# A four-layer graph network on one core: a reordered first chunk, a fixed TensorE order in the third layer, and preparations in steps

## The chip, the core and the metric

The kernel runs on one core of a Trainium2 chip. The metric is device time in microseconds, from launch to end of the core's work; lower is better. The time before is a median of three executions. A core has five engines that run their own instruction streams and meet at semaphores: TensorE (PE in the profile, with its weight loads as PEld), VectorE (DVE), ScalarE (ACT), GpSimd (POOL) and SyncE (SP, which here only starts transfers).

## The reference

Four graph layers in a row on x (4096 nodes, 256 features) with an adjacency matrix adj (4096 x 4096, 0 or 1). Each is followed by a residual sum and a layer norm. Numbered from 0 as in the code:

```python
# layer 0: four heads of 64, additive attention
Wh = (h @ W).reshape(n, heads, d)
e = leaky_relu(s_i[:, None, :] + s_j[None, :, :], 0.2)   # s_i, s_j: Wh with the halves of a
alpha = softmax(where(adj == 0, -inf, e), axis=1)
out = elu(einsum('ijh,jhd->ihd', alpha, Wh))
# layer 1: four heads of scaled dot products, mask from edge.T, then attn @ v
scores = q @ k.T / sqrt(64) + (edge.T - 1) * 10000
# layer 2: as layer 0 with one head, slope 0.01
h = x @ W; e = e_src[:, None] + e_dst[None, :]
out = elu(softmax(where(adj > 0, leaky(e), -1e12), axis=1) @ h)
# layer 3: cosine attention
Qn = cos_normalize(x @ Wq.T); Kn = cos_normalize(x @ Wk.T)
att = softmax(where(adj > 0, Kn @ Qn.T, -9e15), axis=1)
out = 0.5 * (att @ x) + 0.5 * x
# every layer
x = layernorm(x + out)
```

The "third layer" of the change is layer 2.

## The kernel before

All is float32. The 4096 nodes are 32 tiles of 128 (NT) and 8 blocks of 512 (NB, each of QB = 4 tiles). x stays in SBUF as X for the whole kernel and is overwritten layer by layer. A layer first prepares each block (transpose, project, derive the factors), and then goes through units (b, j): for the 512 columns of block b and the neighbours of tile j, it makes attention weights `prob`, masked by adj (loaded on SP two or four tiles at a time), and multiplies them into the block's sums, which lie in PSUM over all 32 j (64 half tiles in layer 1). So a layer is a loop over 256 (512) units, and the preparations are woven into its first block.

**Additive layers (0 and 2).** exp(leaky(s_i + s_j)) is split into factors of i and j: `additive_values` multiplies a transposed block `xT` with the weights (L177), takes three exponentials on ScalarE (L181 to L183: `src`, `dst` and a column of V), and on VectorE writes the projected values, scaled by that column, to V (L184). `src` of a block is laid out as a row over all partitions. A unit is then a Relu on ScalarE of that row with `dst` as the scale (L261, L430), one VectorE instruction that adds 1 and multiplies with the mask (L264, L432), and the matmuls of `sums` (L274, L438).

**transposed_block** turns the four tiles of a block with TensorE into two PSUM banks (L118), which one copy each brings to SBUF (L120). `turn(b)` calls it.

**Layer 0's start** (in `additive_heads`). TensorE's order is the order in the code (`tc.manual_schedule`); the other engines' orders are made by the framework's planner from the same program order, its costs and what is ready. PSUM has two banks `g` from `bank()`, and two accumulators of three banks: `over` and `side`. `warm(2)` issues two products that nothing reads (L339). The row of `a` is spread over partitions in `side` (L342), and `attach` (VectorE, L108 and L110) extends the weights by it. Then come turn(0), warm(2) again, prepare(0) with tiles 0 to 2 in `side` and tile 3 in a bank, and the four rows of block 0 as transposes of broadcast columns (`first_rows`, L234) into a bank and the three banks of `over`. Unit 0's Relu reads the rows from PSUM, and `keep_rows` copies them to SBUF (L239, two on ScalarE, two on VectorE). turn(1) goes into two banks of `side`. The loop makes weights for unit i and sums for unit i - 2 (LAG = 2). After i = 0 stand turn(2) and prepare(1); after i = 3, 7, ... the next turn and preparation. The first sums need an accumulator, which takes the place of `over`. turn(b) also starts the load of x's block b + 2.

**Layer 1** ends with row sums collected in `den`: GpSimd adds even units' weights (L623), its DMA queue accumulates odd ones (L629), and `join_sums` (L646) adds the three parts. The last block's end is `tail`, which layer 2 calls with its own PSUM banks: joins on GpSimd, row sums by TensorE (L658) and copies of them (L661), transposes back (L666 for row sums, L673 for values), reciprocals, residual and layer norm.

**Layer 2** (`additive_one`). Four banks `g` and four accumulators acc0 to acc3; even blocks use the accumulators for their sums, odd blocks four `g`. Blocks 0 and 1 are prepared ahead of the loop; their rows are made by transposes (L420) and a copy (L421), those of later blocks by a trip through DRAM on GpSimd's queue (L415, L416). After weights j = 2, 6, ... of block 0 follow the turn and the preparation of the next block. Sums stand one unit behind weights. Layer 1's tail comes after the sums of unit 2. No engine has a fixed order here: the planner sets TensorE's too. `take_all` divides a finished block's sums, `outputs` finishes it in the next block.

**Layer 3** (`cosine_attention`) needs, for each block, normalised rows turned into T: `Cosine.prepare` turns the block, multiplies each tile with both weight matrices (L795, two tiles to a PSUM bank), takes squares with a running sum on ScalarE (L799), copies rows (L801), computes the inverse root, scales on VectorE (L806), transposes (L810) and copies to T (L811). Six of the eight are done during layer 2's last block, after j = 2, 6, ..., 22, in the banks acc0 to acc3 (`even_bank` gives them in turn), two during layer 3's first block. Its units are L834 (scores), L837 and L838 (exponential, mask) and L845 (sums).

Of the kernel before, what the change touches and what calls it, by code (L numbers as in the profile page):

```python
# [14 lines left out]
OP = mybir.AluOpType  # L15
# [13 lines left out]
def kernel(  # L29
# [140 lines left out]
    def additive_values(xT, b, groups, w_sb, V, src, dst, H, slope):  # L170

        g = 1.0 - slope
        heads = "p k (h d) -> p k h d"
        for k, n, pw in groups:
# [8 lines left out]
            nc.scalar.activation(V[:, t, D:], d, AF.Exp, scale=slope)  # L183
            nc.vector.tensor_tensor(V[:, t, :D].rearrange(heads, h=H), pw[:, :, :D].rearrange(heads, h=H),  # L184
# [12 lines left out]
    def additive_heads(a, H, slope, early, narrow, ahead):  # L197
# [7 lines left out]
        with ExitStack() as lay:  # L205
# [110 lines left out]
            def turn(b, bank=bank):  # L316
                if b + 2 < NB:
                    load_x(b + 2)
                busy = (nc.scalar.copy if b == 0 else nc.vector.tensor_copy,
                        nc.vector.tensor_copy if b == 1 else nc.scalar.copy)  # L320
                xTs[b] = transposed_block(sb, bank, b, busy)

            def prepare(b):
                groups = [(0, HC + 1, side), (HC + 1, 1, bank().rearrange("p (n f) -> p n f", n=1))]
                additive_values(xTs[b], b, groups, w_sb, V, src, dst, H, slope)
# [4 lines left out]
            with tc.manual_schedule(engines={mybir.EngineType.PE}):  # L330
# [14 lines left out]
                warm(2)  # L345
                prepare(0)
                banks = [bank()] + [over[:, h, :] for h in range(H - 1)]
                first_rows(banks)
                free = iter([side[:, 0, :], side[:, 1, :]])
                turn(1, lambda: next(free))  # L350
                for i in range(len(units) + LAG):
                    if i < len(units):
                        b, j = units[i]
                        weights(b, j, None if i else banks)
                        if (b, j) == (1, 4 * QB):
                            early()
                        if i % 8 == 4:
                            narrow(prob[b, j][:, 0, :1])
# [6 lines left out]
                    if i == 0 or i % QB == 3 and 3 + i // QB <= NB:  # L365
                        b = 1 if i == 0 else 2 + i // QB
# [15 lines left out]
    def additive_one(w_sb, slope, tail, op, follow):  # L382
# [3 lines left out]
        with ExitStack() as lay:  # L386
# [21 lines left out]
            def prepare(b, xT):  # L408
                groups = [(k, 1, bank().rearrange("p (n f) -> p n f", n=1)) for k in range(QB)]
                additive_values(xT, b, groups, w_sb, V, src, dst, 1, slope)  # L410
                part = row[:, b * QW:(b + 1) * QW]
# [47 lines left out]
            for b, xT in enumerate([turn(0), turn(1)]):  # L459
                prepare(b, xT)  # L460
            even = itertools.count()
            units = [(b, j) for b in range(NB) for j in range(NT)]
            for i in range(len(units) + 1):
                if i < len(units):
                    b, j = units[i]
                    weights(b, j)
                    if b == 0 and j % QB == 2 and j // QB + 2 < NB:
                        prepare(j // QB + 2, turn(j // QB + 2))
                if i:
                    b, j = units[i - 1]  # L470
                    sums(b, j)
                    if (b, j) == (0, 2):
                        tail(bank)
                        follow.start()
                    if b and j % 4 == 0 and j // 4 < QB:
                        outputs(b - 1, j // 4)
                    if b == NB - 1 and j in (6, 10, 14):
                        follow.load_mask(0, (j - 6) // 4, prob[b, j][:, :1])

                    if b == NB - 1 and j % 4 == 2 and j // 4 < NB - 2:  # L480
                        follow.prepare(even_bank, j // 4)
                    if j == NT - 1:
                        take_all(b)
# [7 lines left out]
    def multi_head_attention(w_sb, b_sb, tail, rows_of_den, narrow_edges):  # L491
# [12 lines left out]
        with ExitStack() as lay:  # L504
# [126 lines left out]
            def sums(b, j):  # L631
# [7 lines left out]
                if j == NH - 1:  # L639

                    kept[b] = [fin1.tile([P, QW], FP, name=f"kept{c}") for c in range(KC + 1)]
# [6 lines left out]
            def row_sums(bank, b):  # L648


                pds = [bank() for _ in range(KC)]
# [93 lines left out]
        def tail(bank):  # L745
            b = NB - 1
            join_sums(b, 1, nc.gpsimd)
            join_sums(b, 2, nc.gpsimd)
            row_sums(bank, b)
            reciprocals(turned_row_sums(bank, b), b)  # L750
            for k in (0, 2):
                half(turned_half(bank, b, k), b, k)
            mv = fin.tile([P, QB, 2], FP, name="mv")
            for k in range(QB):
                one_row(mv, k, X[:, b * QB + k, :D])
            layernorm_block(b, mv)
# [3 lines left out]
    class Cosine:  # L760
# [3 lines left out]
        def __init__(self, stack):  # L764
            self.stack = stack

# [17 lines left out]
        def prepare(self, bank, b):  # L784

            in_, w_sb, T = self.pool, self.w_sb, self.T
            xT = transposed_block(in_, bank, b)
            norm = in_.tile([P, QB, 2], FP, name="norm")
            rows = in_.tile([P, QB, 2, P], FP, name="rows")
            for k in range(QB):  # L790
                t = k % 2
                if t == 0:
                    pr = bank().rearrange("p (t n f) -> p t n f", t=2, f=P)
                for c in range(KC):
                    nc.tensor.matmul(pr[:, t, :, :], xT[:, c, k * P:(k + 1) * P], w_sb[:, c, :],  # L795
                                     start=(c == 0), stop=(c == KC - 1))
                for n in range(2):
                    sq = in_.tile([P, P], FP, name="sq")
# [171 lines left out]
```

## Time and profile before

| | us |
|---|---|
| median of three executions (2927.59 to 2929.03) | 2928.59 |
| the profiled execution | 2932.88 |
| its span, first to last instruction | 2931.0 |

| window, us | what runs | PE busy | DVE | ACT | POOL |
|---|---|---|---|---|---|
| 0 to 20 | layer 0's start | 16.88 | 6.84 | 8.02 | 0.70 |
| 20 to 40 | its first sums | 18.85 | 19.81 | 20.00 | 1.05 |
| 200 to 400 | layer 0's loop | 200.00 | 191.69 | 193.58 | 17.81 |
| 900 to 920 | layer 1's loop | 20.00 | 14.11 | 12.54 | 19.02 |
| 1724.5 to 1743.9 | layer 2's start | 17.48 | 11.67 | 10.20 | 5.51 |
| 2160 to 2237.8 | layer 2's last block, six preparations | 77.47 | 43.91 | 42.37 | 3.54 |
| 2246.8 to 2300 | layer 3's first units, two preparations | 52.78 | 27.80 | 20.83 | 2.96 |
| 2800 to 2931 | the end | 122.96 | 44.05 | 28.62 | 5.92 |

A row of a timeline gives the start, the length, engine, line, operation and the number of like instructions merged into it; in brackets is the idle time before it and what ended that. A float32 matmul appears as two instructions, a transpose as one. An instruction's end is modelled for TensorE and reaches past the start of the next by some 0.2 us, so lengths of neighbouring rows overlap; the distance from one row's start to the next is the time that it held the engine. Busy time therefore also holds short waits between instructions.

### The profile page before, as it was taken

The page shows a single profiled execution, that of the slowest core. Times are in us where ns is not written, and L with a number is a line of the kernel's source. Part 1 is how long each engine was busy: PE and PEld are TensorE (multiplying, and loading weights), DVE is VectorE, ACT ScalarE, POOL GpSimd, SP SyncE. Part 2 cuts the span into 40 slices and gives each one's busy share as a digit, 9 for nine tenths or more (in the row PEclk, how much of TensorE's full clock was granted, in tenths as well). Part 3 has the DMA queues.
Part 4 walks back from the last instruction along what each step waited for, and adds up shares of the span by engine and source line. Part 5 has one row for each costly group of instructions (what it writes and reads, how often), then busy time and mean ns, then how long its engine had stood idle before and what let it go on. Part 6 is the DMA issues. An engine that isn't in the chain of part 4 may idle for free.

```text
span 2931.0 us, 50407 instructions
## 1 busy us (share of the span) xinstructions
PE 2909.7 (99%) x20269; PEld 1560.3 (53%) x20269; DVE 1958.3 (67%) x2545; ACT 1668.9 (57%) x2613; POOL 926.6 (32%) x647
## 2 busy tenths in 40 slices
PE   9999999999999999999999999999999999999998
PEld 4333333333643333333333358888887777777776
DVE  8899999997677777877877865555555333333333
ACT  7899999997356666666666654444444222222222
POOL 0010010100078888888889850000000000000000
PEclk9999999999999999999999999999999999999999
DMA  7566666664068888889889876444442333333331
GB/s 203 102 138 139 136 141 141 137 131 84 1 147 191 183 185 190 182 185 195 176 187 188 180 161 137 151 152 151 154 132 52 51 58 58 58 58 58 58 58 29
DMA packets 207148, 374.94 MB, mean 128 GB/s; under 512 B 15057, under 2 KB 90817, under 8 KB 206018
## 3 DMA queue, kind: packets, MB, share of 16 engines
q0 software_dynamic: 102304, 177.77, 38.3%
q1 hardware_dynamic: 104336, 193.69, 20.1%
q8 instruction: 159, 2.61, 0.4%
q14 instruction: 75, 0.61, 0.1%
q10 hardware_dynamic: 274, 0.26, 0.0%
HBM read 317.07 MB, written 21.04 MB: 115 GB/s over the span
## 4 chain that ended last, share of the span: by engine, by line
PE 96%; DVE 2%; ACT 0%; DMA 0%; SPq 0%; issue 0%; DVEq 0%; ACTq 0%
PE acc L274 23%; PE acc L845 15%; PE p L604 14%; PE acc L637 14%; PE g L438 8%; PE acc L438 8%; PE p L834 4%; PE g L834 3%; PE g L532 2%; PE g L177 1%; PE pv L546 1%; PE acc L795 1%; PE g L118 1%; DVE prob L616 1%; DVE s L139 1%; PE acc L177 1%
## 5 line engine op out<-in xcount | busy, mean ns | idle before, releaser
L616 DVE TENSOR_TENSOR prob<-p,mask 128x1024 f32<-128x1024 f32 x512 | 622.8, 1222 | 197.4 <-ACT p L606 193.6
L606 ACT ACTIVATE p<-p,shift 128x1024 f32<-128x1024 f32 x512 | 556.3, 1088 | 331.8 <-PE p L604 331.0
L274 PE MATMUL acc<-prob,V 128*32 128x512 f32 x6144 | 664.0, 592 | 1.1 <-DVE prob L264 1.1
L623 POOL TENSOR_TENSOR den<-den,prob 128x1024 f32<-128x1024 f32 x248 | 618.5, 2494 | 72.1 <-DVE prob L616 62.7
L261 ACT ACTIVATE prob<-row,dst 128x512 f32<-128x512 f32 x1020 | 633.1, 712 | 0.1
L264 DVE SCALAR_TENSOR_TENSOR prob<-prob,mask 128x2048 f32<-128x2048 f32 x256 | 582.4, 2286 | 24.2 <-ACT prob L261 20.6
L604 PE MATMUL p<-qT,kT 64*64 64x512 f32 x4096 | 532.7, 591 | 5.5 <-DVE prob L616 5.5
L637 PE MATMUL acc<-prob,V 64*64 64x512 f32 x4096 | 531.4, 589 | 0.0
L845 PE MATMUL acc<-X,prob 128*128 128x257 f32 x2048 | 486.0, 380 | 0.0
L845 PEld LDWEIGHTS acc<-X,prob 128*128 128x128 f32 x2048 | 388.4, 190 | 162.2 <-issue 113.5
L838 DVE TENSOR_TENSOR prob<-prob,mask 128x512 f32<-128x512 f32 x256 | 176.3, 691 | 419.5 <-ACT prob L837 418.4
L274 PEld LDWEIGHTS acc<-prob,V 128*32 128x32 f32 x6144 | 197.3, 110 | 453.0 <-issue 433.5
L91 POOL COPY tick<-prob 128x1 f32<-128x1 f32 x35 | 39.7, 1133 | 1019.9 <-DVE prob L264 646.0
L430 ACT ACTIVATE e<-row,dst 128x512 f32<-128x512 f32 x256 | 184.3, 721 | 241.2 <-DVE prob L432 208.4
L637 PEld LDWEIGHTS acc<-prob,V 64*64 64x64 f32 x4096 | 155.8, 133 | 285.4 <-issue 278.2
L604 PEld LDWEIGHTS p<-qT,kT 64*64 64x64 f32 x4096 | 153.6, 133 | 284.4 <-issue 255.8
L432 DVE SCALAR_TENSOR_TENSOR prob<-e,mask 128x512 f32<-128x512 f32 x256 | 178.3, 696 | 174.7 <-PE acc L438 92.9
L782 POOL DMA_DIRECT2D mask<-in_adjT x64 | 47.4, 741 | 639.5 <-DVE prob L838 509.7
L629 POOL DMA_DIRECT2D den<-prob x240 | 225.2, 938 | 28.5 <-DVE prob L616 21.9
L837 ACT ACTIVATE prob<-p 128x512 f32<-128x512 f32 x144 | 85.8, 596 | 256.7 <-PE p L834 242.7
L438 PE MATMUL g<-V,prob 128*128 128x257 f32 x1024 | 226.6, 380 | 0.0
L438 PE MATMUL acc<-V,prob 128*128 128x257 f32 x1024 | 225.3, 380 | 0.0
(154 smaller groups left out, 1973.7 us busy)
## 6 DMA issues: line engine op xcount, KB each, us to landing
mask<-in_adjT SPq DMA_DIRECT2D x256, 512.0 KB
den<-prob POOLq DMA_DIRECT2D x240, 512.0 KB, 5.3
mask<-edges SPq DMA_DIRECT2D x256, 128.0 KB
mask<-in_adjT POOLq DMA_DIRECT2D x64, 512.0 KB, 5.7
edges<-in_adj POOLq DMA_DIRECT2D x32, 512.0 KB, 9.9
den<-prob SPq DMA_DIRECT2D x16, 512.0 KB
row<-far SPq DMA_DIRECT2D x7, 1024.0 KB
X<-in_x SPq DMA_DIRECT2D x7, 512.0 KB
```

Source lines behind the costliest of these rows:

```text
L261: nc.scalar.activation(z[:, h, :], r, AF.Relu, bias=-1.0, scale=dst[:, j, h:h + 1])
L264: nc.vector.scalar_tensor_tensor(z, z, 1.0, mask[m][:, j % MJ, :].unsqueeze(1).to_broadcast([P, H, QW]), OP.add, OP.mult)
L274: nc.tensor.matmul(acc[b][h * G:(h + 1) * G, n, :], part, prob[b, j][:, h, :], start=(j == 0), stop=(j == NT - 1))
L438: nc.tensor.matmul(acc[b][k][:, :D + 1], prob[b, j][:, k * P:(k + 1) * P], V[:, j, :], start=(j == 0), stop=(j == NT - 1))
L604: nc.tensor.matmul(p[c * d:(c + 1) * d, r, :], kT[half, c, j * d:(j + 1) * d], qT[half, c, cols], start=True, stop=True)
L606: nc.scalar.activation(p, p, AF.Exp, bias=shift)
L616: nc.vector.tensor_tensor(z, p, mask[m][:, j % MJ, :].unsqueeze(1).to_broadcast([P, KC, QW]), OP.mult)
L623: nc.gpsimd.tensor_tensor(to, to, flat, OP.add)
L629: nc.gpsimd.dma_start(to, flat, accum_op=OP.add)
L637: nc.tensor.matmul(acc[b][c][r * d:(r + 1) * d, :], V[half, j, r * d:(r + 1) * d], prob[b, j][half, r, :], start=(j == 0), stop=(j == NH - 1))
L834: nc.tensor.matmul(p, T[:, 0, j * P:(j + 1) * P], T[:, 1, cols], start=True, stop=True)
L845: nc.tensor.matmul(acc[b][k], prob[b, j][:, k * P:(k + 1) * P], X[:, j, :], start=(j == 0), stop=(j == NT - 1))
```

## The change

Three parts. In layer 0, turn(1) moves ahead of prepare(0) and into `over`, the second warm(2) is dropped, prepare(0)'s last tile goes to the third bank of `over`, the first rows take two banks `g` and two of `over`, turn(2) moves from behind unit 0 to behind unit 2's step, and the scaling of chunk 1's values is taken out of its preparation and put behind the weights of unit 1. In layer 2, TensorE's order becomes the program's, each turn moves two units ahead of its projection, the rows are filled in places of their own, and layer 1's tail is split into three calls after the sums of units 0, 3 and 5. Layer 3's preparation is split into three steps (turn; project and normalise; turn back), two and three units apart, and in the second step both tiles of a bank are multiplied before their squares.

```diff
-    def additive_values(xT, b, groups, w_sb, V, src, dst, H, slope):
+    def additive_values(xT, b, groups, w_sb, V, src, dst, H, slope, scaled=True):
...
+        if scaled:
+            scale_values(b, groups, V, H)
+
+    def scale_values(b, groups, V, H):
+        heads = "p k (h d) -> p k h d"
+        for k, n, pw in groups:
+            t = slice(b * QB + k, b * QB + k + n)
             nc.vector.tensor_tensor(V[:, t, :D].rearrange(heads, h=H), pw[:, :, :D].rearrange(heads, h=H),
                                     V[:, t, D:].unsqueeze(3).to_broadcast([P, n, H, D // H]), OP.mult)
...
-                busy = (nc.scalar.copy if b == 0 else nc.vector.tensor_copy,
-                        nc.vector.tensor_copy if b == 1 else nc.scalar.copy)
+                busy = (nc.scalar.copy if b == 0 else nc.vector.tensor_copy, nc.scalar.copy)
...
-            def prepare(b):
-                groups = [(0, HC + 1, side), (HC + 1, 1, bank().rearrange("p (n f) -> p n f", n=1))]
-                additive_values(xTs[b], b, groups, w_sb, V, src, dst, H, slope)
+            def prepare(b, last=None, scaled=True):
+                groups = [(0, HC + 1, side), (HC + 1, 1, last or bank().rearrange("p (n f) -> p n f", n=1))]
+                additive_values(xTs[b], b, groups, w_sb, V, src, dst, H, slope, scaled)
+                return groups
...
                 turn(0)
-                warm(2)
-                prepare(0)
-                banks = [bank()] + [over[:, h, :] for h in range(H - 1)]
+
+                free = iter([over[:, 0, :], over[:, 1, :]])
+                turn(1, lambda: next(free))
+                prepare(0, over[:, HC:, :])
+                banks = [bank(), bank(), over[:, 0, :], over[:, 1, :]]
                 first_rows(banks)
-                free = iter([side[:, 0, :], side[:, 1, :]])
-                turn(1, lambda: next(free))
                 for i in range(len(units) + LAG):
                     if i < len(units):
                         b, j = units[i]
                         weights(b, j, None if i else banks)
+                        if i == 1:
+                            scale_values(1, second, V, H)
...
-                    if i == 0 or i % QB == 3 and 3 + i // QB <= NB:
-                        b = 1 if i == 0 else 2 + i // QB
+
+                    if i == 0:
+                        second = prepare(1, scaled=False)
+                    elif i == 2:
+                        turn(2)
+                    elif i % QB == 3 and 2 + i // QB < NB:
+                        b = 2 + i // QB
                         if b + 1 < NB:
                             turn(b + 1)
                         prepare(b)
...
-            def prepare(b, xT):
-                groups = [(k, 1, bank().rearrange("p (n f) -> p n f", n=1)) for k in range(QB)]
+            def project(b, xT, ks=range(QB)):
+                groups = [(k, 1, bank().rearrange("p (n f) -> p n f", n=1)) for k in ks]
                 additive_values(xT, b, groups, w_sb, V, src, dst, 1, slope)
+
+            def fill_row(b):
                 part = row[:, b * QW:(b + 1) * QW]
...
-            for b, xT in enumerate([turn(0), turn(1)]):
-                prepare(b, xT)
...
+            with tc.manual_schedule(engines={mybir.EngineType.PE}):
+                xTs = {0: turn(0), 1: turn(1)}
+                project(0, xTs[0])
+                project(1, xTs[1], [0, 1])
+                fill_row(0)
+                project(1, xTs[1], [2, 3])
+                for i in range(len(units) + 1):
+                    if i < len(units):
+                        b, j = units[i]
+                        weights(b, j)
+
+                        if b == 0 and j // QB + 2 < NB:
+                            n = j // QB + 2
+                            if j % QB == 0:
+                                xTs[n] = turn(n)
+                            elif j % QB == 2:
+                                project(n, xTs[n])
+                                fill_row(n)
+                    if i:
+                        b, j = units[i - 1]
+                        sums(b, j)
+                        if (b, j) == (0, 1):
+                            fill_row(1)
+                        if b == 0 and j in (0, 3, 5):
+                            tail(bank, (0, 3, 5).index(j))
+                            if j == 5:
+                                follow.start()
+                        if b and j % 4 == 0 and j // 4 < QB:
+                            outputs(b - 1, j // 4)
+                        if b == NB - 1:
+                            if j in (6, 10, 14):
+                                follow.load_mask(0, (j - 6) // 4, prob[b, j][:, :1])
+
+
+                            for step, first in enumerate((0, 2, 5)):
+                                if j >= first and (j - first) % 4 == 0 and (j - first) // 4 < NB - 2:
+                                    follow.prepare(even_bank, (j - first) // 4, step)
+                        if j == NT - 1:
+                            take_all(b)
...
-        def tail(bank):
+        def tail(bank, step):
+
             b = NB - 1
-            join_sums(b, 1, nc.gpsimd)
-            join_sums(b, 2, nc.gpsimd)
-            row_sums(bank, b)
-            reciprocals(turned_row_sums(bank, b), b)
-            for k in (0, 2):
-                half(turned_half(bank, b, k), b, k)
...
+            if step == 0:
+                join_sums(b, 1, nc.gpsimd)
+                join_sums(b, 2, nc.gpsimd)
+            elif step == 1:
+                row_sums(bank, b)
+            else:
+                pd = turned_row_sums(bank, b)
+                pos = {k: turned_half(bank, b, k) for k in (0, 2)}
+                reciprocals(pd, b)
+                for k, po in pos.items():
+                    half(po, b, k)
...
-        def prepare(self, bank, b):
+        def prepare(self, bank, b, step):
...
+            if step == 0:
+                self.xT[b] = transposed_block(in_, bank, b)
+            elif step == 1:
...
+                for k in range(0, QB, 2):
                     pr = bank().rearrange("p (t n f) -> p t n f", t=2, f=P)
...
+                    for t in range(2):
+                        for c in range(KC):
+                            nc.tensor.matmul(pr[:, t, :, :], xT[:, c, (k + t) * P:(k + t + 1) * P], w_sb[:, c, :],
+                                             start=(c == 0), stop=(c == KC - 1))
+                    for t in range(2):
+                        for n in range(2):
+                            sq = in_.tile([P, P], FP, name="sq")
+                            nc.scalar.activation(sq, pr[:, t, n, :], AF.Square, accum_out=norm[:, k + t, n:n + 1])
+                    nc.vector.tensor_copy(rows[:, k:k + 2], pr)
...
+            steps = {(0, j + n): (NB - 2 + b, step) for b, j in enumerate((1, 12)) for step, n in enumerate((0, 2, 5))}
...
-                        co.prepare(bank, NB - 2)
-                    elif (b, j) == (0, 12):
-                        co.prepare(bank, NB - 1)
+                    if (b, j) in steps:
+                        co.prepare(bank, *steps[b, j])
```

## The prediction

> **What bounds the kernel.** I read the busy times first, then what TensorE waited for, then TensorE's timeline at the three places of the change.
>
> ```profile
> PE 2909.7 (99%) x20269; PEld 1560.3 (53%) x20269; DVE 1958.3 (67%) x2545; ACT 1668.9 (57%) x2613; POOL 926.6 (32%) x647
> ...
> PE g L177 <- DVE xT L120: 1.9, 1, 1.9
> PE acc L177 <- issue: 1.2, 1, 1.2
> PE acc L274 <- DVE prob L264: 1.1, 1, 1.1
> ```
>
> TensorE is busy 2909.7 of 2931.0 us, and the chain of waits gives it 96%. The change takes no computing from it except four warming instructions, so all it can win is TensorE's waits: 21.3 us in all, of which some 8 lie after the last matmul (2800 to 2931 us has 122.96 busy) and 5.5 in layer 1 (L604), both untouched. But the timeline models a matmul's end, and merged rows hide short waits; start minus start of successive rows shows them. The first chunk:
>
> ```profile
> 8.85 4.67 PE L177 MATMUL acc<-w_sb,xT 128*128 128x264 f32 x12 [1.19 <-issue]
> 13.36 1.05 PE L177 MATMUL g<-w_sb,xT 128*128 128x264 f32 x4
> ...
> 16.15 1.04 PE L118 MATMUL acc<-ident,X 128*128 128x128 f32 x8
> ...
> 18.57 2.94 PE L177 MATMUL acc<-w_sb,xT 128*128 128x264 f32 x12 [0.51 <-DVE xT L120]
> ...
> 22.32 2.78 PE L274 MATMUL acc<-prob,V 128*32 128x512 f32 x24
> 26.25 2.78 PE L274 MATMUL acc<-prob,V 128*32 128x512 f32 x24 [1.15 <-DVE prob L264]
> ...
> 33.55 0.64 PE L274 MATMUL acc<-prob,V 128*32 128x512 f32 x4
> ```
>
> From the third sum (33.55) TensorE waits for nothing until 680 us, so what the chunk gains before 33.55 shifts all that follows.
>
> **First chunk.** From the end of the first rows (16.15) to 33.55 are 17.40 us. Work in it: three turns of 0.87 (16.15 to 17.02), two preparations of 16 instructions at 0.222 (13.36 to 14.25 is four), 3.55 each, two sums of 2.61 (96 instructions take 10.44): 14.93. So 2.47 are waits: xT's copies, the row copies, prob.
> - *turn(1) moved ahead of prepare(0).* TensorE has a hole from 7.66 to 8.85: L177 writes the bank that attach's second product (DVE, to 8.75) still reads. Its X block is the next transfer after X(0) and w0; 1.3 MB at the measured 280 to 340 GB/s puts it at about 7 us. Eight transposes at half speed (0.21 each, as at 5.26) then end near 9.1: prepare(0) starts 0.25 later, and 0.87 leaves the later stretch. Its two load issues on SP (0.5 each) go ahead of masks first needed near 19 us; cost nothing.
> - *The second warm(2) removed.* Its 1.06 us stood in that hole: nothing by itself.
> - *The clock.* Twelve L177 take 4.51 us here and 2.77 at 18.57: the slow start costs 1.74, and the profile's clock row, which shows full speed, misses it. A rule speaks against the change: the Trainium skill, "TensorE: Matmul & The Clock Gate", Part 4 "PE-mode transpose", says that transposes don't count as activity for the clock gate. By it, warming begins with the L177 as before: 0, and in the worst case, with the two products missed, slow until 16.15, which adds four L177 at 0.22 and 16 transposes at 0.107, +2.6. If transposes do warm, work without a hole from 7 us brings full speed up to 1.85 us earlier: -0.9. The row is nearer the rule (transposes and products from 4.2 to 7.7 had not raised it by 8.85): I take 0.
> - *turn(2) behind the first sum, scaling of chunk 1 behind the second weights.* Work after 16.4 is now 14.06, so without a wait the third sum starts at 30.46 (-3.1). Waits: the four Relu at 0.62 end at 17.8, prob(0,0) takes 2.28 to 20.1, a row copy 0.68 behind it frees the accumulator: first sum at 20.8 (TensorE is there at 19.95). turn(2)'s second bank is the one that the deferred scaling still reads (0.94 and 0.41 on DVE). If DVE scales in the gap before prob(0,1), that is done by 22.1, the turn follows the sum (23.4 to 24.3), prob(0,1) is ready at 24.4, and with 2.61 + 0.87 + 3.55 the third sum starts at 31.5. If prob(0,1) goes first (ScalarE readies it at 21.4: 17.8, two row copies of 0.6, four Relu), scaling ends at 25.0, TensorE stands behind turn(2), and it is 32.5 (-1.1). In before DVE put the scaling first (22.73, then prob at 23.92): I take **-2.0**.
>
> **Start of layer 2 (the diff's third layer).**
>
> ```profile
> 1737.22 1.03 PE L438 MATMUL acc<-V,prob 128*128 128x257 f32 x4
> 1740.11 3.91 PE L177 MATMUL g<-w_sb,xT 128*128 128x258 f32 x16 [1.85 <-DVE xT L120]
> ...
> 1736.55 2.81 DVE L432 SCALAR_TENSOR_TENSOR prob<-e,mask 128x512 f32<-128x512 f32 x1 [1.14 <-PE acc L438]
> 1739.28 0.68 DVE L120 COPY xT<-g 128x512 f32<-128x512 f32 x1
> ...
> 1736.46 2.34 POOL L646 TENSOR_TENSOR den<-den 128x1024 f32<-128x1024 f32 x1 [7.60 <-DMA den<-prob]
> ```
>
> The longest wait: xT(2)'s copy stood on DVE behind a prob of 2.81 us, elsewhere 0.69, held as long as POOL's join of layer 1's row sums ran. With turn(2) at unit 0 and its project at unit 2 the order is project(1) to 1733.75, transposes to 1734.6, copy by about 1735.5, ahead of the join, under sum 0 (1.74 us, to 1736.4). First row: fill_row(0) ends at 1732.0, then ACT copy 0.58, Relu 0.72, prob 0.69 and hand-overs: 1734.3, under project(1)'s last half (1.74) and the turn (0.87); without that cover it would be 2.3. The blocked prob is then prob(0,1) or later, wanted after project(2) at 1739.9. Saved: 1.85 with 0.26 of slow first matmuls, and 0.33 of split fill_row(1): **-2.4** (ends -2.6 and -1.6, if sum 0 waits 0.8).
> A second rule to weigh: the same skill, "SBUF — State Buffer", "Who interferes with whom", has a DVE operation with two SBUF inputs and a GpSimd one shut each other out entirely. The joins move from unit 2 to unit 0; by the rule alone they could now meet prob(0,0), +2.1. The POOL row decides: the second join idled 7.60 us for its DMA, so being asked earlier doesn't move it. I take 0.
> *Tail in steps.* Row sums (16 matmuls, 0.59) now stand behind sum 3, near 1746, in a queue with every later sum behind them; the join ends at 1738.8, so no wait. Transposes come two units (3.5 us) after the kept copies (0.37 each), which stalled TensorE 0.36: **-0.4**. follow.start's two SP loads move from unit 2 to 5; wanted 400 us later: 0. Turns of blocks 3 to 7 go two units ahead of their projections; these already run without a wait.
>
> **Layer 3's preparations.**
>
> ```profile
> 2162.05 3.23 PE L795 MATMUL acc<-w_sb,xT 128*128 128x256 f32 x12
> 2165.12 1.46 PE L438 MATMUL g<-V,prob 128*128 128x257 f32 x6
> 2166.58 1.13 PE L795 MATMUL acc<-w_sb,xT 128*128 128x256 f32 x4
> 2167.54 4.50 PE L438 MATMUL g<-V,prob 128*128 128x257 f32 x20
> ```
>
> At 0.217 an instruction, 12 L795 should take 2.60; to the next row are 3.07 (0.47 lost), then 1.46 for 1.30 (0.16), 0.96 for 0.87 (0.09), and to the transposes at 2172.09 4.55 for 4.34 (0.21); with 0.19 before it 1.12 us. The second preparation (2173.43 to 2185.99) loses 0.81 in the same way, the other four some 0.75 each: 4.9. Its cause: the second tile's matmuls write a bank whose first half the Squares read. Now both tiles are multiplied before the Squares, and each step stands 2 or 3 units (3.5 to 6.1 us) behind its input: copies need 0.7, the root and scaling 4.45 (2167.5 to 2171.95). Step 0 at unit 0 writes acc0 and acc1, free at 2154.74 and 2155.46, before 2156.7. A wait or bank change per step stays, 0.1 each as in L177's runs, 0.25 a preparation: 4.9 - 1.5 = 3.4, taken as **-3.2** (ends -4.3 and -1.6, half). The two preparations inside layer 3 lose 1.0 and 0.6 (2250.34 to 2263.98, 2282.57 to 2293.68): **-1.0**. TensorE's order is not fixed there.
>
> **Sum:** -2.0 - 2.4 - 0.4 - 3.2 - 1.0 = -9.0. The profiled execution takes 2932.88 us with a span of 2931.0; less 9.0 it is 2923.9. It stands 4.3 above the median 2928.59, from which I forecast **2919.6 us**.
>
> **Rivals.**
> - *Half of it stays.* If the first chunk stands behind turn(2) and the small losses belong to every change of operand: 1.1 + 2.0 + 1.6 = 4.7 saved, 2923.9. For it: L177 keeps 0.1 in runs that wait for nothing. Against: the 0.47 are too large for that.
> - *More than that.* Transposes warm (0.9), the chunk runs free (another 1.1), the six preparations give 4.3: 3.1 more, 2916.5. For it: the free sum is 30.46.
> - *Slower: the fixed order makes every unit of layer 2 wait.* Its 256 sums stand one unit behind their weights; a wait costs a first matmul 0.10 us even where it is short. All of them: 26.6 - 9.0, +17.6, 2946.2; it turns slower beyond 0.2% from 143 waiting units. Against: L432's idle of 174.7 us is mostly for L438, so prob is ready as early as three buffers allow.
>
> **How the numbers follow.** A measurement tells 0.2% (5.9 us, below 2922.7) from nothing. Forecast 0.64, half 0.16, more 0.12, slower 0.05, no visible effect 0.03. Faster: 0.64 + 0.12 + 0.04 of the half case = 0.80; same 0.15; slower 0.05. The range reaches from the larger case to the half one: 2916.3 to 2924.6.
>
> **What would show it.** The third L274 group starting near 31.5 instead of 33.55; no wait for xT at the first L177 behind a turn in layer 2; sixteen L795 in one row of about 3.6 us; L666 without its 0.2. Wrong if TensorE waits at turn(2) for the scaling, at layer 2's first sum, or at unit 0 of its last block.

## The result, and the profile after

| | before | after | ratio after/before (95%) |
|---|---|---|---|
| first group, 6 runs each: median (lowest to highest), us | 2928.45 (2927.59 to 2930.18) | 2920.95 (2918.87 to 2921.23) | 0.9973 (0.996 to 0.9986) |
| later, on another chip, 22 and 5 runs | 2930.39 (2928.39 to 2932.99) | 2919.40 (2918.30 to 2921.02) | 0.9963 (0.9951 to 0.9976) |
| the profiled execution, us | 2932.88, span 2931.0 | 2920.96, span 2918.0 | |

The forecast was 2919.6 us with a range of 2916.3 to 2924.6. The kernel is faster, by 7.5 us in the first group and 11.0 in the second, where the steps added up to 9.0. The total is right, but the parts are not: they missed in both directions, and the runs below say which. So the closeness of the total is partly luck.

First the page of the changed kernel, its row of busy times, then what TensorE waited for (engine, line and buffer; releaser; us in total, times, longest):

```profile
PE 2900.7 (99%) x20265; PEld 1564.3 (54%) x20265; DVE 1957.0 (67%) x2544; ACT 1668.5 (57%) x2614; POOL 928.3 (32%) x647
```
```profile
PE p L635 <- DVE prob L647: 5.6, 8, 0.8
...
PE acc L280 <- DVE row L245: 1.0, 1, 1.0
```

The span is 13.0 us shorter, but TensorE's idle time fell only from 21.3 to 17.3 (2918.0 - 2900.7). The other 9.0 us left the *busy* time, with four instructions fewer. Slow first matmuls, matmuls at a low clock and stalls inside a merged row all count as busy, so a list of waits would have shown less than a third of this gain. Of the waits shown before, xT's 1.9 us at the projection is gone; layer 1's eight waits (now L635) are what they were.

TensorE's timeline of the first chunk in the changed kernel (start, busy time, line, what is computed; the sums are now at L280, the projections at L176):

```profile
7.41 1.97 PE L118 MATMUL acc<-ident,X 128*128 128x128 f32 x8 [0.40 <-DMA X<-in_x]
9.17 4.84 PE L176 MATMUL acc<-w_sb,xT 128*128 128x264 f32 x16
...
20.52 2.78 PE L280 MATMUL acc<-prob,V 128*32 128x512 f32 x24 [1.01 <-DVE row L245]
23.24 1.10 PE L118 MATMUL g<-ident,X 128*128 128x128 f32 x8
24.26 2.78 PE L280 MATMUL acc<-prob,V 128*32 128x512 f32 x24
...
31.56 8.79 PE L280 MATMUL acc<-prob,V 128*32 128x512 f32 x80
```

The third sum starts at 31.56, against 33.55 before and 31.5 forecast. One wait is left, 1.01 us ahead of the first sum, for the last row copy.

The same view where layer 2 starts (sums L453), and in its last block (layer 3's preparations L836):

```profile
1732.70 1.90 PE L453 MATMUL acc<-V,prob 128*128 128x257 f32 x8
1734.44 3.66 PE L176 MATMUL g<-w_sb,xT 128*128 128x258 f32 x16
1737.93 1.90 PE L453 MATMUL acc<-V,prob 128*128 128x257 f32 x8
```
```profile
2167.36 3.62 PE L836 MATMUL acc<-w_sb,xT 128*128 128x256 f32 x16
2170.81 3.63 PE L453 MATMUL g<-V,prob 128*128 128x257 f32 x16
```

In both, the next row starts when the work of the one before is done: 16 L176 in 3.49 us, 16 L836 in 3.45. The sixteen L836 were rows of 12 and 4 with sums between; now they are one row and cost 0.216 us each, what they cost with nothing lost.

For every profile I took the length of each stage, from the start of TensorE's first instruction in it to the first of the next. "Full clock" is the time of the trace's clock record, from which an L177 (L176) takes 0.22 us instead of 0.44. In e_chunk and e_pairs layer 2 has the order of before; the experiments are described below.

| profile | full clock from | first weights start | third sum starts | layer 2 to its last block | last block | layer 3 |
|---|---|---|---|---|---|---|
| before | 12.43 | 8.85 | 33.55 | 430.40 | 91.98 | 684.15 |
| before again (e_before) | 9.10 | 7.67 | 31.31 | 430.15 | 91.99 | 684.04 |
| after | 11.42 | 9.17 | 31.56 | 426.54 | 86.71 | 682.14 |
| after again (e_after) | 8.77 | 8.82 | 30.09 | 426.54 | 86.71 | 682.14 |
| e_chunk | 10.39 | 9.12 | 31.02 | 428.30 | 91.99 | 684.09 |
| e_rest | 9.14 | 8.05 | 31.53 | 426.54 | 86.71 | 682.29 |
| e_rest_again | 12.76 | 9.03 | 33.81 | 426.54 | 86.71 | 682.14 |
| e_pairs | 9.55 | 7.95 | 31.68 | 428.29 | 90.35 | 683.35 |
| e_unpaired | 10.46 | 8.95 | 30.97 | 426.54 | 101.93 | 682.91 |
| e_late_turn | 11.35 | 9.22 | 31.55 | 428.25 | 86.71 | 682.14 |
| e_no_fixed | 13.89 | 9.68 | 33.03 | 426.54 | 86.71 | 682.14 |
| e_turn1_back | 9.01 | 7.86 | 31.21 | 426.54 | 86.71 | 682.14 |
| e_rows_scaled | 11.02 | 9.11 | 31.41 | 426.54 | 86.71 | 682.14 |

The stages behind the first chunk repeat to 0.15 us wherever the program and its waits are the same. From the third sum to layer 2 all profiles take 1690.96 to 1691.07 us, but for e_before (1691.55, with 0.6 more of waits in layer 1), so what the chunk gains is kept. The first chunk itself does not repeat.

### The profile page after: what moved, and what is told of

It reads as the page before. It is cut to its first block, busy times and chain, and to the rows that moved or that the text cites. A ratio compares the mean times of both kernels' runs of the same rounds, so it can differ in the third digit from the quotient of the medians.

```text
span 2918.0 us, 50372 instructions
## 1 busy us (share of the span) xinstructions
PE 2900.7 (99%) x20265; PEld 1564.3 (54%) x20265; DVE 1957.0 (67%) x2544; ACT 1668.5 (57%) x2614; POOL 928.3 (32%) x647
## 4 chain that ended last, share of the span: by engine, by line
PE 98%; DVE 2%; ACT 0%; DMA 0%; issue 0%; SPq 0%; DVEq 0%; ACTq 0%
PE acc L280 23%; PE acc L888 15%; PE p L635 15%; PE acc L668 14%; PE acc L453 8%; PE g L453 8%; PE p L877 4%; PE g L877 3%; PE g L563 2%; PE g L176 1%; PE pv L577 1%; PE acc L176 1%; PE g L118 1%; PE acc L836 1%; DVE prob L647 1%; DVE s L139 1%
## 5 line engine op out<-in xcount | busy, mean ns | idle before, releaser
L280 PE MATMUL acc<-prob,V 128*32 128x512 f32 x6144 | 664.0, 592 | 1.0 <-DVE row L245 1.0
L635 PE MATMUL p<-qT,kT 64*64 64x512 f32 x4096 | 532.8, 590 | 5.6 <-DVE prob L647 5.6
L280 PEld LDWEIGHTS acc<-prob,V 128*32 128x32 f32 x6144 | 197.3, 110 | 452.2 <-issue 434.1
L445 ACT ACTIVATE e<-row,dst 128x512 f32<-128x512 f32 x256 | 184.2, 721 | 232.8 <-DVE prob L447 206.6
L635 PEld LDWEIGHTS p<-qT,kT 64*64 64x64 f32 x4096 | 153.8, 133 | 284.4 <-issue 255.7
L453 PE MATMUL g<-V,prob 128*128 128x257 f32 x1024 | 225.6, 380 | 0.0
L453 PE MATMUL acc<-V,prob 128*128 128x257 f32 x1024 | 225.1, 380 | 0.0
```

The costliest lines, as they stand in the source:

```text
L280: nc.tensor.matmul(acc[b][h * G:(h + 1) * G, n, :], part, prob[b, j][:, h, :], start=(j == 0), stop=(j == NT - 1))
L453: nc.tensor.matmul(acc[b][k][:, :D + 1], prob[b, j][:, k * P:(k + 1) * P], V[:, j, :], start=(j == 0), stop=(j == NT - 1))
L635: nc.tensor.matmul(p[c * d:(c + 1) * d, r, :], kT[half, c, j * d:(j + 1) * d], qT[half, c, cols], start=True, stop=True)
```

## The experiments

**Before, once more.** The same kernel, to see which of its rows belong to the program and which to one execution.

> The kernel before once more, for a second profile of it. The first profiled execution was 4.4 us above the median, and stage by stage it is 13.0 us longer than the profile of after, where the medians differ by 7.5. If the losses belong to the program, this profile shows them again: a prob of some 2.8 us behind the join, 0.47 lost in the first twelve L795 of a preparation, 522 us from layer 2's first transpose to layer 3's first score, and a span near 2931. If the first profile caught a chance (the join meeting a prob), the blocked prob and its 1.85 us wait are gone, and the span is near 2926.5.

It took 2930.91 us, with a span of 2929.0, between the two that were expected. Rows of its first chunk on TensorE's timeline:

```profile
7.67 3.62 PE L177 MATMUL acc<-w_sb,xT 128*128 128x264 f32 x12 [0.15 <-issue]
...
24.02 2.78 PE L274 MATMUL acc<-prob,V 128*32 128x512 f32 x24 [1.15 <-DVE prob L264]
...
31.31 1.92 PE L274 MATMUL acc<-prob,V 128*32 128x512 f32 x16
```

The third sum is at 31.31 here, not 33.55, in the same program. The first weights started 1.18 us sooner, and twelve of them took 3.45 us instead of 4.51, since the clock rose at 9.10 instead of 12.43. So 33.55, from which the prediction counted, was a late start. The wait at layer 2's start, in contrast, came back. First VectorE, then GpSimd, then TensorE in this run:

```profile
1734.90 2.56 DVE L432 SCALAR_TENSOR_TENSOR prob<-e,mask 128x512 f32<-128x512 f32 x1 [1.14 <-PE acc L438]
1737.38 0.68 DVE L120 COPY xT<-g 128x512 f32<-128x512 f32 x1
```
```profile
1734.55 2.35 POOL L646 TENSOR_TENSOR den<-den 128x1024 f32<-128x1024 f32 x1 [7.27 <-DMA den<-prob]
```
```profile
1738.20 3.91 PE L177 MATMUL g<-w_sb,xT 128*128 128x258 f32 x16 [1.60 <-DVE xT L120]
```

The prob ends at 1737.46, 0.56 us after the join (1736.90); the copy starts behind it; TensorE waits 1.60.

**The first chunk alone.** Layers 2 and 3 are those of before; only the diff's part in additive_values and additive_heads is kept.

> Only the first chunk is changed. Forecast's step: third sum near 31.5 us instead of 33.55, -2.0 us, 2926.4. If TensorE stands behind turn(2): -1.1. If the shift is lost later in layer 0 or 1, the third sum is early and the time as before.

2929.15 us (2927.51 to 2933.10), ratio 0.9996 (0.9988 to 1.0004): 1.3 us by the means, 1.6 by the medians, not told from nothing. Its layer 2 start shows something else. VectorE, then GpSimd:

```profile
1734.13 0.69 DVE L445 SCALAR_TENSOR_TENSOR prob<-e,mask 128x512 f32<-128x512 f32 x1 [1.14 <-PE acc L451]
1734.74 0.68 DVE L120 COPY xT<-g 128x512 f32<-128x512 f32 x1
```
```profile
1734.72 2.35 POOL L659 TENSOR_TENSOR den<-den 128x1024 f32<-128x1024 f32 x1 [7.86 <-DMA den<-prob]
```

Here the join came 0.59 us *after* the prob started, which took its usual 0.69, and the projection waits for nothing. That is why this stage takes 428.30 and not 430.15, with layer 2 as in before: whether the 1.6 to 1.9 us are lost hangs on when one DMA lands. Of four profiles with this layer 2, two lost them (e_pairs, below, did not).

**Layers 2 and 3 alone.** The first chunk is that of before.

> Only layers 2 and 3 are changed. Forecast's steps: -2.4 - 0.4 - 3.2 - 1.0 = -7.0, 2921.4. If the stages of the two profiles are taken at their word: -11, 2917.4. From the measured 7.5 in all, less 2.0 for the chunk: -5.5, 2923.

2919.80 us (2918.89 to 2920.24), ratio 0.9962 (0.9949 to 0.9976). This is 11.0 below before, what the stages of the two profiles said, so nearly the whole gain lies here. VectorE at layer 2's start, then TensorE:

```profile
1732.89 0.68 DVE L120 COPY xT<-g 128x512 f32<-128x512 f32 x1
...
1735.01 2.51 DVE L434 SCALAR_TENSOR_TENSOR prob<-e,mask 128x512 f32<-128x512 f32 x1 [0.25 <-ACT e L432]
```
```profile
1732.62 1.90 PE L440 MATMUL acc<-V,prob 128*128 128x257 f32 x8
1734.36 3.66 PE L177 MATMUL g<-w_sb,xT 128*128 128x258 f32 x16
```

A prob is held here too (2.51 us), but the copy of xT went 2 us before it, and TensorE loses nothing. The collision is still there; what moved is the work that stood behind it.

**Pairing alone.** Before, with one edit in Cosine.prepare; no steps, no hand-written order:

```diff
-            for k in range(QB):
...
+            for k in range(0, QB, 2):
...
+                for t in range(2):
+                    for c in range(KC):
...
+                for t in range(2):
+                    for n in range(2):
+                        sq = in_.tile([P, P], FP, name="sq")
+                        nc.scalar.activation(sq, pr[:, t, n, :], AF.Square, accum_out=norm[:, k + t, n:n + 1])
```

> Before, with one edit: both tiles of a bank are multiplied ahead of their Squares; the preparation stays one call and TensorE's order the planner's. If the bank that the Squares read is the cause, the first eight L795 of a preparation run without loss, some 0.5 us for each of eight preparations: -3 to -4. If the losses come from the weaving of sums between them, or from every change of operand: 0 to -1.

2927.76 us (2926.32 to 2929.45), ratio 0.999 (0.9983 to 0.9996). The last block is shorter by 1.64 us (91.99 to 90.35), layer 3 by another 0.7: 2.3, where 3 to 4 were expected. TensorE's timeline of the last block:

```profile
2158.10 3.98 PE L794 MATMUL acc<-w_sb,xT 128*128 128x256 f32 x16
2161.91 6.23 PE L438 MATMUL g<-V,prob 128*128 128x257 f32 x28
...
2170.46 3.80 PE L794 MATMUL acc<-w_sb,xT 128*128 128x256 f32 x16
```

The sixteen are in one row, yet it takes 3.98 and 3.80 us, not 3.62, and this run's list of waits has four for the scaled rows at the transposes back:

```profile
PE acc L809 <- DVE rows L805: 0.9, 4, 0.2
```

The steps still stand too close to what they read. Of the 5.28 us that the whole change wins in this block, pairing by itself gives 1.64; the other 3.64 came only with the steps set apart as well.

**The whole change and e_rest again**, side by side on another chip.

> The whole change once more, beside its second part alone on the same chip. If the chunk's 2.0 us add to the rest: 2.0 below the second part alone. If they came from the first profile's late w0 (prepare(0) began at 8.85 there, at 7.67 to 8.05 in three later profiles of the same chunk, at 9.12 and 9.17 behind the moved turn(1)): within 1 us of it.

> Second part alone, on the same chip as the whole change. It was 11.0 below before in the last group; expected again 9 to 11 below before, and either 2 above the whole change (chunk adds) or within 1 us of it (chunk gives nothing).

2919.40 (2918.30 to 2921.02) and 2920.00 us (2919.17 to 2922.00), ratios 0.9963 (0.9951 to 0.9976) and 0.9964 (0.9951 to 0.9978): the first chunk's new order shows as 0.6 us between these two, which lies within their scatter. TensorE at the start of the whole change's second profile:

```profile
5.53 1.54 PE L118 MATMUL g<-ident,X 128*128 128x128 f32 x6 [0.63 <-DMA X<-in_x]
7.11 1.88 PE L118 MATMUL acc<-ident,X 128*128 128x128 f32 x8
8.82 3.73 PE L176 MATMUL acc<-w_sb,xT 128*128 128x264 f32 x16
12.38 1.19 PE L240 MATMUL g<-ident,src 128*128 128x128 f32 x8
```

The sixteen L176 take 3.56 us, full speed from the first; in the other profile of this program (9.17 to 13.85) they take 4.68.

**turn(1) back behind the first rows**, in the new chunk. It should start prepare(0) sooner and keep the rest.

```diff
-                free = iter([over[:, 0, :], over[:, 1, :]])
-                turn(1, lambda: next(free))
+                warm(2)
                 prepare(0, over[:, HC:, :])
...
+                free = iter([side[:, 0, :], side[:, 1, :]])
+                turn(1, lambda: next(free))
```

(The copies of xT for block 1 are both on VectorE again.)

> The whole change, but turn(1) goes back behind the first rows (into side, both copies on VectorE) with warm(2) in the hole again; turn(2) stays behind the first sum. If waiting for X's second block ahead of prepare(0) is what eats the chunk's gain, prepare(0) begins near 8.0 instead of 9.15 and the third sum near 30.5: 0.5 to 1 below the whole change. If turn(1)'s place in the hole is what gains: 0.9 above it.

2920.09 us (2919.42 to 2920.75), ratio 0.9965 (0.9952 to 0.9977): no better than e_after (2919.40). TensorE's timeline:

```profile
7.86 4.36 PE L176 MATMUL acc<-w_sb,xT 128*128 128x264 f32 x16 [0.26 <-issue]
...
16.42 2.94 PE L176 MATMUL acc<-w_sb,xT 128*128 128x264 f32 x12 [1.38 <-DVE xT L120]
...
31.21 5.36 PE L280 MATMUL acc<-prob,V 128*32 128x512 f32 x48
```

prepare(0) does start at 7.86, and the gain is spent at once: prepare(1) waits 1.38 us for xT, whose copies are back on VectorE's path. Either order has one wait of over 1 us, the other one ahead of the first sum.

**Squares directly behind each tile's matmuls**, with the steps and their distances as changed (the two loops over t are one again).

> The whole change, but in a preparation's second step each tile's Squares follow its matmuls again, so the bank's second tile waits for the first one's Squares, now with TensorE's order fixed. If that bank is the cause of the losses: twice some 0.6 to 0.7 us for each of six preparations, +7 to +8, and a little in layer 3. If the distance between the steps did it: within 1 us of the whole change.

2935.62 us (2934.55 to 2936.86), ratio 1.0016 (1.0009 to 1.0023): this one edit turns the gain into a loss. The waits, then TensorE's timeline of one preparation:

```profile
PE acc L836 <- ACT sq L840: 12.0, 12, 1.3
```
```profile
2168.74 1.03 PE L836 MATMUL acc<-w_sb,xT 128*128 128x256 f32 x4
2171.05 2.00 PE L836 MATMUL acc<-w_sb,xT 128*128 128x256 f32 x8 [1.28 <-ACT sq L840]
2173.82 1.13 PE L836 MATMUL acc<-w_sb,xT 128*128 128x256 f32 x4 [0.77 <-ACT sq L840]
```

The second tile's matmuls stand until ScalarE has squared the first's, twice in a preparation. From 2168.74 to the next row (2174.79) are 6.05 us where 3.45 are work: 2.6 lost, by six preparations 15.6, and the stage is 15.2 longer. I had expected half of that. The named waits (1.28 + 0.77) are 2.05 of the 2.6. Of the rest, 0.2 are the two first matmuls behind a wait (each holds TensorE for 0.32 us instead of 0.22), and some 0.33 are the ends of the matmuls ahead of the waits, which are modelled too late and so count as busy. In before, the order that the planner had found put sums between the tiles (the rows of 12, 6, 4, 20), and the whole loss was 0.88 a preparation. That it is the fixed order that takes this cover away is likely but not shown: no run has this edit with the order left to the planner.

**The order not fixed in layer 2.** The program text stays in its new order; the planner orders TensorE's work again.

```diff
-            with tc.manual_schedule(engines={mybir.EngineType.PE}):
+            with nullcontext():
```

> The whole change, but in layer 2 TensorE's order is left to the planner again; turns, rows, tail and preparation steps stay where the change puts them. If fixing the order matters for itself: the losses of layer 2's last block come back in part, 2 to 4 us above the whole change. If the placing of the steps in the program did it: within 1 us of it.

2920.41 us (2919.04 to 2922.05), ratio 0.9965 (0.9952 to 0.9979), and the same 426.54, 86.71 and 682.14 us. With the steps in these places, fixing TensorE's order earns nothing more; the places in the program do it.

**turn(2) right ahead of project(2)** instead of two units before:

```diff
-                            if j % QB == 0:
+                            if j % QB == 0 and n > 2:
                                 xTs[n] = turn(n)
                             elif j % QB == 2:
+                                if n == 2:
+                                    xTs[n] = turn(n)
                                 project(n, xTs[n])
```

> The whole change, but turn(2) of layer 2 stands right ahead of project(2) again, with TensorE's order fixed. Forecast's step: the distance between turn and projection is the gain. TensorE then waits for xT(2)'s copies, at least 0.8 us, and up to 2.9 where the copy stands behind a prob that the join holds: 1 to 3 above the whole change. If the distance is worth nothing: no wait for xT in layer 2 and the same time.

2921.67 us (2920.15 to 2922.73), ratio 0.997 (0.9959 to 0.9982); the stage is 1.71 longer. TensorE at layer 2's start:

```profile
1732.35 2.00 PE L453 MATMUL acc<-V,prob 128*128 128x257 f32 x8 [0.41 <-DVE prob L447]
1734.18 1.04 PE L118 MATMUL g<-ident,X 128*128 128x128 f32 x8
1735.89 3.85 PE L176 MATMUL g<-w_sb,xT 128*128 128x258 f32 x16 [0.67 <-ACT e L445]
```

Without the transposes ahead of it the first sum waits 0.41 us for prob. The projection waits 0.67 us while the copies of its xT stand behind other work: VectorE's behind a prob (copy to 1735.74), ScalarE's behind the Relu L445 that the row names (copy to 1736.37). The join met no prob here, so this is the price of the short distance without a collision. That before without one lost as much (1.76) is chance: there it lay in other rows, which are added up below.

**The last wait of the first chunk.** The third row copy goes to VectorE, the fourth to ScalarE, and the scaling is not put off:

```diff
-(nc.vector.tensor_copy if h % 2 else nc.scalar.copy)(row[0][:, h, :], banks[h])
+(nc.vector.tensor_copy if h in (1, 2) else nc.scalar.copy)(row[0][:, h, :], banks[h])
```

> A try at more: the whole change with the third row copied on VectorE and the fourth on ScalarE, so that the first sum no longer stands behind a row copy that follows prob(0,0) on VectorE (a wait of 1.01 us in three profiles); the scaling stays in the preparation, which leaves the order as it is. If that copy is what the first sum waits for: the wait falls to 0.4 or less and the third sum comes 0.5 earlier; too little to see in the time. If prob(0,0) is then later by as much: nothing.

2920.31 us (2919.17 to 2921.62), ratio 0.9966 (0.9953 to 0.9978): nothing. The first sum in TensorE's timeline:

```profile
20.38 2.78 PE L280 MATMUL acc<-prob,V 128*32 128x512 f32 x24 [1.10 <-DVE prob L270]
```

The wait is as long as before the edit and only has another name: prob(0,0) itself is now last, since the copy went ahead of it on VectorE. The two follow each other on one engine, and swapping them leaves the end of the second where it was.

## Why the prediction was right, and where it was not

- **First chunk, -2.0: the mechanism held, the size did not.** The first sum came at 20.52 (20.8 forecast), the third at 31.56 (31.5), VectorE scaled before prob(0,1), and TensorE never stood behind turn(2). But the sum was made against one late start. Up to the full clock the work goes at half speed (0.44 us for an L177 instead of 0.22), so both the start of the first weights and the time of full clock count half. Over the profiles the third sum follows, to 0.05 us, 22.94 + half the start of the first weights + half the time of full clock in the old chunk, and 21.27 + the same halves in the new one (a fit to five and six profiles; where full clock precedes the start, the start counts twice). So the new order is 1.67 us shorter at the same start and clock. In e_turn1_back the constant is 22.78 (31.21 less half of 7.86 and half of 9.01), so nearly all of the 1.67 comes with the move of turn(1) and its copies. The term that was mis-sized is *"prepare(0) starts 0.25 later"*, counted from one late start (8.85): in the five profiles of the old chunk prepare(0) started at 7.67 to 9.03 (mean 8.31), in the six of the new one at 8.82 to 9.68 (mean 9.16), since turn(1) needs X's second block first. Half of these 0.85 us counts, which leaves 1.2 at the same clock; the timings show 0.6 (e_after against e_rest_again) to 1.6 (e_chunk) and can't tell it from nothing.
- **The clock, 0.** The prediction followed the Trainium skill ("TensorE: Matmul & The Clock Gate", Part 4 "PE-mode transpose"), which has transposes not count as activity. The measurement speaks against it for these float32 transposes: in e_after the products ended at 4.28, only transposes ran from there to 8.8, and the first L176 already took 0.22 us. It is one profile of its kind. The gain of 0.9 counted for that case can't be told from the scatter of the full clock's time, 8.8 to 13.9 us.
- **Start of layer 2 and the tail, -2.8: measured -3.6 to -3.9** where before's join met a prob, -1.76 where it didn't. The cause was as told: the copy of xT behind a held prob. The order came as forecast too (transposes, sum 0, then project(2) without a wait), and the joins moved to unit 0 cost nothing. The tail's transposes follow their row without a stall (L698 at 1752.19, 1.73 after the sum before it). The starts of successive rows in before, less the work in them, give the parts of the 3.86: 2.27 at project(2) (2.11 forecast), 0.43 at the split rows (0.33), 0.47 at the transposes back (0.4), and 0.67 in a term that the prediction put at nothing, *"Turns of blocks 3 to 7 go two units ahead of their projections; these already run without a wait"*. Four of these projections (blocks 4 to 7) lost 0.17 us each, inside a merged row. One of them in before, then one in the changed kernel:

```profile
1765.55 3.83 PE L177 MATMUL g<-w_sb,xT 128*128 128x258 f32 x16
1769.21 6.23 PE L438 MATMUL acc<-V,prob 128*128 128x257 f32 x28
```
```profile
1759.58 3.65 PE L176 MATMUL g<-w_sb,xT 128*128 128x258 f32 x16
1763.07 3.63 PE L453 MATMUL acc<-V,prob 128*128 128x257 f32 x16
```

The same sixteen take 3.66 us there and 3.49 here. Without the collision project(2) lost only 0.16 (e_chunk), and the parts are 1.76 again. The prediction also lacked that the collision doesn't happen in every execution.
- **Layer 3's six preparations, -3.2: measured -5.3.** The failing term is *"A wait or bank change per step stays, 0.1 each ... 0.25 a preparation"*: nothing stays, 16 L836 take 3.45 us. The loss in before was 0.88 a preparation (5.28 by six), near the 0.8 read from the rows. The split was not foreseen: pairing 1.64, distance 3.64.
- **The two preparations in layer 3, -1.0: measured -1.9 to -2.0** (684.04 and 684.15 to 682.14). The prediction's own reading of 1.0 and 0.6 lost was nearer than the amount it took.
- **The rivals.** *Slower by waits at every unit* did not happen: L453 runs in a row of 256, a whole block, without a wait (from 1816.06, 55.68 us). *Half of it stays* is refuted for layers 2 and 3; for the chunk its number fits, but not its reason, since TensorE didn't stand behind turn(2). *More than that* was nearest on the preparations (4.3).

Added up with the chunk at 1.2, the stages give 10.2 us (no collision in before) to 12.3 (with one). The second group's 11.0 lies among them. The first group's 7.5, with an interval of 4.1 to 11.7, reaches into them at its upper end. The forecast counted its losses in a profile with a late start and a collision, and took them off a median 4.3 us lower, which may hold less of both; that most terms were sized too small made up for it. This is the luck in the total. Why before's median was 2928.45 in one group and 2930.35 to 2930.77 in three later ones stays open; how often the join collides and when the clock rises in unprofiled executions would both bear on it, and neither is seen there. What deferring the scaling does by itself wasn't tried.

## What to carry to other kernels

Profile the kernel to be changed twice before counting from the time of one row: in the first tens of microseconds the arrival of a transfer and the clock's rise moved the same row by 2.2 us, more than the edit there won. Start minus start of successive rows, against the work in them, finds losses that the list of waits doesn't have; here they were most of the gain. When an order is written out, put two or three units between a step and its input and multiply everything that shares an accumulator before the first reader of it is issued. Here fixing the order added nothing to that (e_no_fixed), and with the order fixed and the steps apart, but without the pairing, the last block took 15 us longer (e_unpaired).

## What the hardware showed that was not expected

- Full speed of TensorE came between 8.77 and 13.89 us in kernels whose instructions up to there are nearly the same, and each microsecond of it costs half a microsecond at the third sum (30.09 to 33.81 over all profiles). The granted clock of the profile doesn't show it: for before it reads 1.00 from 4 to 8 us too, where a transpose takes 0.21 us instead of 0.11. The slow start is seen only in the length of the instructions.
- The records of full clock differ in length between the traces by whole multiples of 3.413 us (2901.33, 2904.74, 2911.57, 2914.98, 2918.40), so the clock seems to change in steps of that length. Where the steps lie against the kernel's start differs between executions: the two profiles of the changed kernel have the rise 2.65 us apart, which is no whole step. In the two of before it lies 3.33 apart, close to one step; that the late weights cost a whole step there is likely, but not shown.
- VectorE's two-input operation and GpSimd's hold each other up both ways. If the join came first, prob took 2.51 to 2.85 us instead of 0.69 (eight profiles); where a prob was just ahead, the join took 2.75 to 2.79 instead of its 2.35 (three profiles). The first profile of the changed kernel is one of the three:

```profile
1735.26 2.75 POOL L677 TENSOR_TENSOR den<-den 128x1024 f32<-128x1024 f32 x1 [7.88 <-DMA den<-prob]
```

- Behind a wait, the first float32 matmul holds TensorE for 0.32 us instead of 0.22 and counts as busy. In e_unpaired, where the program has TensorE wait at a semaphore for the Squares of the bank's first half, twelve named waits of 0.72 to 1.28 us (12.0 in all) made the stage 15.2 us longer. The wait is the program's; no run shows what the chip would do without it.
